# Moving the first LoRA factors to GpSimd's queue, with block 1's loads behind block 0's on the other two

## The chip, the cores and the metric

The kernel runs on one core of one Trainium2 chip. The time is the device time of one execution in microseconds (us). A core has five engines that run their own instruction streams and wait for one another on semaphores: TensorE (PE, matrix products; its weight loads are listed as PEld), VectorE (DVE), ScalarE (ACT), GpSimd (POOL) and SyncE (SP). SP, ACT and POOL can request transfers between the chip's memory and the on-chip buffer; the transfers run on the core's 16 DMA engines. A request by SP or ACT is listed under SPq or ACTq.

## The reference

The input x has 2 sequences of 1024 tokens with 512 features. It is normalized over the features, passed through a state-space convolution along the features and, in parallel, through a gated feed-forward network with LoRA factors; their product is added to x. Cut to what matters here:

```python
xn = layernorm(x)                                    # over the 512 features
s  = s4_convolution(xn) + D * xn
h1 = xn @ w1.T + 2 * (xn @ A1.T) @ B1.T              # hidden size 1376, rank 16
h3 = xn @ w3.T + 2 * (xn @ A3.T) @ B3.T
h2 = silu(h1) * h3
g  = silu(h2 @ w2.T + 2 * (h2 @ A2.T) @ B2.T)
out = x + s * g
```

Everything is fp32.

## The kernel before

The 2048 tokens are cut into 4 blocks of 512 (TB), each of 4 tiles of 128 tokens (NTT). The hidden size 1376 is cut into 5 pairs of 256 columns and a last piece of 96 columns (LASTR). The large products run as block products of a fast matrix multiplication with 7 instead of 8 partial products on two levels, so sums and differences of weights and tokens are made on DVE and POOL, and PE runs chains of products, almost all at line L801.

The LoRA factors are not applied to the tokens. PE multiplies the factors A and B with each other (`lora_product`, L412), and the result times 2 is added to the weights (`merge`, L422, for a pair; `take_last` and `merge_last`, L522 and L530, for the last piece). The weights so merged then meet the tokens.

The order of the work is written out by hand: each engine runs its instructions in the order in which the program names them. Requests of transfers also run in the order of their queue. A request on SP or ACT takes one of eight semaphores in turn, so the ninth waits until the first has landed, and so on.

The start of the program, in the order of its lines:

- `load_x(0)` (L232, L238): the four tiles of block 0, 256 KB each, alternating between SP's queue (tiles 0 and 2) and ACT's (tiles 1 and 3).
- POOL clears `warm` and builds the identity `ident`, which PE needs for transposes.
- `load_lora` (L398 to L403) for the two factor pairs: each requests A (`lo_d`, 16 rows of 512) at L401 and columns 768 to 1375 of B (`lo_h`, 16 rows of 608) at L402. The first pair goes to SP's queue, the second to ACT's.
- ACT runs an activation on `warm` (L1031), which loads its function table.
- `load_x(1)`: the four tiles of block 1, all on SP's queue.
- POOL builds a triangle `tri`, used much later.
- SP's queue: the last piece of the weights (`load_last`, L504), pair 0 (`load_pair`, L431), blocks 2 and 3, pair 1, and a second copy of the factors.

Then the work: PE runs 18 + 18 products of the identity (`keep_warm`, L1049) and after them the LoRA products of the last piece (`lora_last`, into the y banks) and half of those of pair 0. ACT scales the first (L522). DVE takes the statistics of block 0 tile by tile (L254, L255), and makes the reciprocal root (L59 to L68) and the shift (L291). ACT normalizes tiles 0 and 2 (L300), POOL tiles 1 and 3 (L304). POOL then adds the scaled LoRA products to the last piece (L530). PE transposes block 0 (L311), ACT copies it out (L319), and the first chain runs on the last piece (L801). The same steps follow for block 1: statistics on DVE, normalization on ACT and POOL, transposes (L331). On ACT, L522 stands before L300; on DVE, block 1's statistics stand right behind block 0's shift.

Of the kernel before, what the change touches and what calls it, by code (L numbers as in the profile page):

```python
# [21 lines left out]
HID = 1376  # L22
# [11 lines left out]
LSPLIT = 6 * P  # L34
# [75 lines left out]
def s4_gated_ffn(  # L110
# [39 lines left out]
    nc = tc.nc  # L150
# [66 lines left out]
    def value(tag="s"):  # L217
        return upool.tile([P, TB], F32, tag=tag, name=tag, bufs={"s": 8, "c": 4}[tag])
# [13 lines left out]
    def load_x(b):  # L232
        room = (None, None, t_in[4], t_in[6])[b]
        tiles = []
        for tt in range(NTT):
            t = value() if room is None else room[:, tt, :]
            queue = nc.scalar if b == 0 and tt % 2 else nc.sync
            queue.dma_start(out=t, in_=x[bass.ds(b * TB + tt * P, P), :])  # L238
            tiles.append(t)
        return tiles  # L240
# [157 lines left out]
    def load_lora(queue, group, d, h, lo, hi):  # L398
        rows = slice(32 * group, 32 * group + R)
        if d is not None:  # L400
            queue.dma_start(out=lora["d"][rows, :], in_=d)  # L401
        queue.dma_start(out=lora["h"][rows, : hi - lo], in_=h[:, lo:hi])  # L402
        lora["base"][group] = lo  # L403
# [607 lines left out]
    def add_chain(n, ch, places=PLACES):  # L1011
# [8 lines left out]
        for i, p in places:  # L1020
            at(7 * n + p, lambda i=i: step(i))

    x_in = {0: load_x(0)}
    warm = const.tile([P, 1], F32, name="warm")
    nc.gpsimd.memset(warm, 0.0)
# [1 line left out]
    lora_tiles(LSPLIT)  # L1027
    factors = (a1, b1T), (a3, b3T)
    for v, f in enumerate(factors):
        load_lora((nc.sync, nc.scalar)[v], v, *f, LSPLIT, HID)  # L1030
    nc.scalar.activation(warm, warm, AF.Silu)  # L1031
    x_in[1] = load_x(1)
    make_upper_triangular(nc, tri, 1.0, diag=True)
    w_last, s_last = load_last()
    w_pair, s_pair = {0: load_pair(0)}, {c: {} for c in range(NPAIR)}
    x_in[2], x_in[3] = load_x(2), load_x(3)
    w_pair[1] = load_pair(1)
    for v, f in enumerate(factors):
# [90 lines left out]
    for n in range(4):  # L1129
        half, v = 1 - n // 2, n % 2  # L1130
# [19 lines left out]
    for n, place in enumerate((10.7, 11.7, 13.7, 14.4)):  # L1150
        b, i = divmod(n, 2)
# [517 lines left out]
```

## Time and profile before

| what | value |
|---|---|
| median of 3 runs | 437.12 us (437.03 to 437.62) |
| the profiled execution's own time | 437.84 us |
| its span (first to last instruction) | 435.8 us |
| PE busy | 429.5 us, 99% of the span |
| DVE, POOL, ACT busy | 324.0, 210.8 and 146.4 us |
| moved by DMA | 53.60 MB, mean 123 GB/s |

The profile is one execution; its time is 2.04 us above its span, and 0.72 us above the median of the runs. Times in it count from the start of the span. A row of the timeline gives the start, the busy time, the engine, the line, the operation, the tiles written and read, the shapes and the number of instructions merged; in brackets stands the idle time just before and what ended it. A row of the chain of waits gives the start, the duration and the work that the end depended on. A row of DMA issues ends with the size and the time from the request to the landing. A row of stretches gives the granted clock, then for PE, PEld, DVE, ACT and POOL the busy time and the number of instructions, the clock again, the mean busy share of the 16 DMA engines and GB/s.

In the first 36 us the transfers are dense: the DMA engines are busy 80 to 100% of the time from about 2 to 24 us.

### The profile page before, as it was taken

The numbers are of one execution on the slowest core, as the hardware profiler recorded it, in microseconds if no ns is written. First come the engines' busy times: TensorE is split into PE (matmuls) and PEld (weight loads), VectorE is DVE, ScalarE is ACT, GpSimd is POOL, SyncE is SP. The second block draws the span as 40 slices with busy tenths as digits, with TensorE's granted clock in tenths as the row PEclk, the third lists the DMA queues.
The fourth block names the chain that finished last, engine by engine and source line by source line (L and its number), as shares of the span: only waits on it lengthen the run. The fifth ranks groups of instructions, "written<-read, shape, count | busy, mean of one in ns | idle before, by whom it ended". The sixth has DMA issues, their size and how long they took to land.

```text
span 435.8 us, 5085 instructions
## 1 busy us (share of the span) xinstructions
PE 429.5 (99%) x1664; PEld 270.6 (62%) x1664; DVE 324.0 (74%) x531; ACT 146.4 (34%) x301; POOL 210.8 (48%) x159
## 2 busy tenths in 40 slices
PE   7999999999999999999999999999999999999996
PEld 7645334444444444444443447888898999989996
DVE  5989998995894789478946788879786885753234
ACT  2897243443254325432543242211101212112221
POOL 1629186699689467946794478300000123222221
PEclk9999999999999999999999999999999999999999
DMA  7930313026015101521154554495902832423211
GB/s 242 367 100 21 137 49 101 0 73 194 25 37 170 60 25 46 167 67 31 49 157 158 168 166 154 125 352 194 350 2 78 307 118 96 146 96 98 74 72 48
DMA packets 35465, 53.60 MB, mean 123 GB/s; under 512 B 4688, under 2 KB 21520, under 8 KB 35312
## 3 DMA queue, kind: packets, MB, share of 16 engines
q1 hardware_dynamic: 31824, 49.55, 34.1%
q10 hardware_dynamic: 3616, 3.74, 2.9%
q8 instruction: 13, 0.21, 0.2%
q14 instruction: 12, 0.10, 0.1%
HBM read 33.88 MB, written 19.40 MB: 122 GB/s over the span
## 4 chain that ended last, share of the span: by engine, by line
PE 88%; DVE 8%; ACT 1%; DMA 1%; issue 1%; POOL 0%; SPq 0%; DVEq 0%; ACTq 0%; POOLq 0%
PE x L801 43%; PE y L801 23%; PE w L801 12%; PE aux L982 2%; PE w L982 2%; PE aux L997 2%; DVE xt L357 2%; DMA s<-in_x_dram 1%; DVE s L487 1%; PE y L412 1%; DVE w L475 1%; PE y L574 1%; PE aux L756 1%; ACT c L261 1%; DVE aux L1384 1%
## 5 line engine op out<-in xcount | busy, mean ns | idle before, releaser
L1387 POOL TENSOR_TENSOR o<-o,xin 128x512 f32<-128x512 f32 (+1 forms) x17 | 23.3, 1368 | 132.7 <-DVE o L1386 132.7
L887 POOL TENSOR_TENSOR s<-c,s 128x512 f32<-128x512 f32 (+1 forms) x44 | 67.0, 1526 | 20.1 <-ACT c L879 17.5
L821 ACT COPY s<-x 128x512 f32<-128x512 f32 (+1 forms) x54 | 31.6, 586 | 76.4 <-PE x L801 72.1
L801 PE MATMUL x<-t_in,s 128*128 128x512 f32 (+1 forms) x148 | 55.5, 495 | 0.0
L825 DVE TENSOR_TENSOR s<-s,y 128x512 f32<-128x512 f32 (+1 forms) x54 | 36.5, 681 | 15.3 <-ACT s L821 8.4
L921 POOL TENSOR_TENSOR s<-ua_three,s 128x512 f32<-128x512 f32 x20 | 35.0, 1751 | 14.7 <-DVE s L825 14.7
L801 PEld LDWEIGHTS x<-t_in,s 128*128 128x128 f32 x148 | 27.6, 190 | 20.9 <-issue 17.9
L801 PE MATMUL y<-t_in,s 128*128 128x256 f32 (+1 forms) x108 | 36.4, 461 | 0.0
L921 POOL TENSOR_TENSOR ua_three<-ua_three,s 128x512 f32<-128x512 f32 x20 | 29.5, 1477 | 12.3 <-DVE s L825 12.3
L1409 ACT COPY z<-x 128x256 f32<-128x256 f32 x24 | 8.8, 372 | 69.6 <-PE x L801 69.5
L1384 DVE TENSOR_TENSOR aux<-aux,m 128x384 f32<-128x384 f32 x32 | 18.1, 565 | 15.7 <-PE aux L982 14.1
L921 POOL TENSOR_TENSOR s<-u_three,s 128x512 f32<-128x512 f32 x20 | 26.7, 1333 | 3.7 <-DVE s L825 1.8
L801 PEld LDWEIGHTS y<-t_in,s 128*128 128x128 f32 x108 | 19.8, 190 | 11.7 <-issue 7.3
L879 ACT ACTIVATE c<-c 128x512 f32<-128x512 f32 x40 | 24.1, 630 | 8.9 <-DVE c L921 8.9
L844 ACT COPY w<-x 128x512 f32<-128x512 f32 (+1 forms) x37 | 21.1, 571 | 15.7 <-PE x L801 15.7
L475 DVE TENSOR_TENSOR w<-w 128x512 f32<-128x512 f32 x20 | 22.5, 1138 | 0.1
L921 POOL TENSOR_TENSOR u_three<-ua_three,u_three 128x512 f32<-128x512 f32 x10 | 13.0, 1302 | 16.9 <-DVE u_three L825 15.5
L801 PE MATMUL x<-xt,w 128*128 128x512 f32 x40 | 20.6, 597 | 0.0
L801 PE MATMUL x<-xr,w 128*128 128x512 f32 x40 | 20.6, 597 | 0.0
L801 PE MATMUL x<-xr,s 128*128 128x512 f32 x40 | 20.4, 596 | 0.0
L801 PE MATMUL x<-xt,s 128*128 128x512 f32 x40 | 20.4, 592 | 0.0
L801 PE MATMUL x<-t_in,w 128*128 128x512 f32 x40 | 20.4, 592 | 0.0
(321 smaller groups left out, 922.0 us busy)
## 6 DMA issues: line engine op xcount, KB each, us to landing
g_dram<-s SPq DMA_DIRECT2D x40, 256.0 KB, 2.1
g<-g_dram SPq DMA_DIRECT2D x10, 512.0 KB, 6.4
xin<-in_x_dram SPq DMA_DIRECT2D x16, 256.0 KB, 2.8
out_dram<-o SPq DMA_DIRECT2D x14, 256.0 KB, 2.0
t_in<-g_dram SPq DMA_DIRECT2D x6, 512.0 KB, 4.2
t_in<-in_x_dram SPq DMA_DIRECT2D x8, 256.0 KB, 5.5
w_a<-in_w2T_dram SPq DMA_DIRECT2D x2, 1024.0 KB, 7.1
room<-g_dram SPq DMA_DIRECT2D x4, 512.0 KB, 5.6
```

Source lines behind the costliest of these rows:

```text
L475: nc.vector.tensor_tensor(*sums[name])
L801: nc.tensor.matmul(ps[:, cols], lhsT=lhsT, rhs=rhs if parts == 1 else rhs[:, cols], start=first and i == 0 and part == 0, stop=i == len(pa ...
L821: nc.scalar.copy(t, self.x)
L825: nc.vector.tensor_tensor(t, t, self.y, add)
L844: nc.scalar.copy(self.w, self.x)
L879: nc.scalar.activation(c, c if src is None else src, AF.Silu)
L887: nc.gpsimd.tensor_tensor(g, act, g, mult)
L921: (nc.vector if o < 20 else nc.gpsimd).tensor_tensor(to, a, b, add)
L982: nc.tensor.matmul(to[:, n * P : (n + 1) * P], lhsT=x_, rhs=by, start=start, stop=True, skip_group_check=True,)
L1384: nc.vector.tensor_tensor(y[:, P:], y[:, P:], m[:, n * P : (n + 3) * P], add)
L1387: (nc.vector if last else nc.gpsimd).tensor_tensor(o, o, self.xin[h][:, cols], add)
L1409: nc.scalar.copy(t, xb)
```

## The change

Three edits, all at the start of the program. The two pairs of factors are requested on POOL's queue, behind the identity and before the triangle. Block 1's four tiles are requested alternately on SP's and ACT's queue, like block 0's. `load_x(1)` is placed before the activation on `warm`, so that ACT's two requests for block 1 stand before its table load. The order on PE and DVE is the same; on POOL four requests are added; on ACT two requests of factors are replaced by two of block 1; on SP two requests of factors and two of block 1 are gone, and those of block 1 that remain follow block 0's without a wait, since with fewer requests before them they take free semaphores.

```diff
@@ load_x
-            queue = nc.scalar if b == 0 and tt % 2 else nc.sync
+            queue = nc.scalar if b < 2 and tt % 2 else nc.sync
@@ after make_identity
     lora_tiles(LSPLIT)
     factors = (a1, b1T), (a3, b3T)
     for v, f in enumerate(factors):
-        load_lora((nc.sync, nc.scalar)[v], v, *f, LSPLIT, HID)
-    nc.scalar.activation(warm, warm, AF.Silu)
+        load_lora(nc.gpsimd, v, *f, LSPLIT, HID)
     x_in[1] = load_x(1)
+    nc.scalar.activation(warm, warm, AF.Silu)
     make_upper_triangular(nc, tri, 1.0, diag=True)
     w_last, s_last = load_last()
```

More of the change, by code (lines that the diff above doesn't have):

```diff
@@ L1029, in s4_gated_ffn @@
     for v, f in enumerate(factors):
-        load_lora((nc.sync, nc.scalar)[v], v, *f, LSPLIT, HID)
+        load_lora(nc.gpsimd, v, *f, LSPLIT, HID)
+    x_in[1] = load_x(1)
     nc.scalar.activation(warm, warm, AF.Silu)
-    x_in[1] = load_x(1)
     make_upper_triangular(nc, tri, 1.0, diag=True)
```

## The prediction

> **What bounds the kernel now.** First the page: its shares say who is busy, its chain who sets the end.
>
> ```profile
> span 435.8 us, 5085 instructions
> PE 429.5 (99%) x1664; PEld 270.6 (62%) x1664; DVE 324.0 (74%) x531; ACT 146.4 (34%) x301; POOL 210.8 (48%) x159
> PE 88%; DVE 8%; ACT 1%; DMA 1%; issue 1%; POOL 0%; SPq 0%; DVEq 0%; ACTq 0%; POOLq 0%
> ```
>
> TensorE (PE) is the bound, 88% of the chain; transfers hold 1%. Nearly all loads of this kernel are hidden, so the diff can pay only where PE has not yet begun its unbroken run. I looked for that place in the timeline, and then followed the chain of waits of the first 21 us.
>
> ```profile
> 7.82 1.04 PEld L412 LDWEIGHTS y<-lo_h,lo_d 16*128 16x128 f32 x15 [0.22 <-issue]
> 8.98 0.87 ACT L522 ACTIVATE c<-y 128x384 f32<-128x384 f32 x2 [4.90 <-PE y L412]
> 10.31 1.52 ACT L300 ACTIVATE s<-s,shift,rs_y 128x512 f32<-128x512 f32 x2 [0.46 <-DVE shift L291]
> 11.18 1.09 PE L311 MATMUL aux<-ident,s 128*128 128x128 f32 x8 [1.15 <-ACT s L300]
> 18.76 1.02 PE L801 MATMUL w<-xr,last 128*96 128x512 f32 x2
> 20.47 1.88 PE L801 MATMUL y<-xt,last 128*96 128x512 f32 x4
> ```
>
> From 18.76 on PE starts a 512-column product every 0.43 us (two rows later, at 20.47, four begin 1.71 after two pairs), with gaps of tenths only. So the end is 18.76 plus a nearly fixed 417 us, and the change is worth what it moves 18.76. Back from there PE is also dense down to 11.18, where it had idled 1.15 us for ScalarE's (ACT's) normalization of block 0. That began at 10.31, and two strands meet in it.
>
> ```profile
> 1.16 5.41 DMA s<-in_x_dram
> 6.59 0.71 DVE stats L254
> 10.12 0.17 DVE shift L291
> 10.31 0.82 ACT s L300
> ```
>
> Strand one, which ends last: block 0's third tile releases VectorE (DVE) at 6.59; from there to the shift's end is a fixed 3.70 us of small operations (6.59 to 10.29). Strand two: the first LoRA factors, which L412 multiplies from 7.82; L522 on ACT waits for them and ends at 8.98 + 0.87 = 9.85, and since ACT runs in order L300 stands behind it. The slack of this strand is 10.31 - 9.85 = 0.46 us. Their landings:
>
> ```profile
> s<-in_x_dram ACTq DMA_DIRECT2D x1, 256.0 KB, 5.7
> lo_d<-in_a_dram ACTq DMA_DIRECT2D x1, 32.0 KB, 5.9
> lo_h<-in_b3T_dram ACTq DMA_DIRECT2D x1, 38.0 KB, 5.8
> ```
>
> The last factor is requested at 2.11 and lands 5.8 later, at 7.91, which is where PE begins L412. PE's weight loads had been free since 7.82 - 0.22 = 7.60, when the warming products ran out: earlier factors gain 0.2 us at most.
>
> **What is removed.** Four factor requests leave the two hardware queues (0.42 to 0.45 us of issue each). The third tile of block 0 should profit. The stretches of one microsecond show why it is late:
>
> ```profile
> 4.00:5.00 1.00, 1.00 (x7) 1.00 (x7) 0.97 (x3) 0.08 (x1) 0.00 (x0) 1.00 1.01 357
> 5.00:6.00 1.00, 1.00 (x7) 1.00 (x7) 0.59 (x2) 0.00 (x0) 0.00 (x0) 1.00 0.70 93
> 6.00:7.00 1.00, 1.00 (x12) 1.00 (x11) 0.41 (x1) 0.00 (x0) 0.00 (x0) 1.00 1.04 232
> ```
>
> The last two columns are the DMA engines' share and GB/s. Stretches 1 to 5 us carried 43, 371, 385 and 357 GB/s, 1.16 MB in all; block 0 is 1.05 MB. So its bytes had mostly moved by 5.0, yet the release came at 6.57, after a stretch in which the engines were 70% busy for 93 GB/s. In that stretch the factors' rows (16 partitions, 0.14 MB) are what stands behind block 0 on both queues. If they are the reason, up to 6.59 - 5.63 = 0.96 us can go (5.63 is when DVE has finished the first two tiles); if not, nothing. I take half: 0.5, so the release is at 6.1 and the shift ends at 9.8.
>
> **What is added.** Four requests on GpSimd (POOL), in order after the identity's last operation, which ends at 1.02 + 0.29 = 1.31; two operations for the triangle stand behind them and are needed much later, and POOL's next work is at 10.38. The trace has no POOL request. Below, the issue is bounded by the hardware queues' 0.43 us; above by the longest mean POOL row, 1.75 us (L921, 128x512). From issue to landing, below: 1.9 us, the median of the late 48 KB factors on a quiet queue; above: 5.8, theirs now, behind block 0. On a queue of their own they stand behind nothing, so I take 2.1 near the lower end, and 1.1 for the issue, the middle of its bounds. The last factor then lands at 1.31 + 4 x 1.1 + 2.1 = 7.8: L412 starts at 7.8, L522 ends 2.0 later (7.85 to 9.85 now), at 9.8, and the slack holds. The bounds run from 1.31 + 1.7 + 1.9 = 4.9 (held by PE's 7.60) to 1.31 + 7.0 + 5.8 = 14.1.
>
> [...]
>
> **What is moved.** Block 1's four requests stand fifth to eighth in line. Now they wait for block 0's landings and leave SP between 3.91 and 7.39; then they leave both queues by about 2.5 (two requests ended at 1.57 to 1.60, two more take 0.9). ACT still issues four requests before its table load at 2.59, so the warm activation does not move. Block 1's bytes follow block 0's: 2.1 MB at the 371 GB/s of the second stretch, from 2.0, is 7.7, some 9 with a landing delay of 1; DVE first needs them at 10.20 - 0.5 = 9.7. Covered by DVE's own 3.70 us on block 0; without that cover it would cost microsecond for microsecond.
> On SP the two "last" loads (L504) then wait for tiles 0 and 1 and go near 4 instead of 7.43, the weights, blocks 2 and 3 and the second pair up to 3 us sooner. No engine's wait in the first 36 us ends on any of them, so I price this at nothing; the cover is POOL's normalization, which ends at 11.91 while the "last" pieces land at 11.3 and 12.0. A faster start would have eaten that cover; the earlier requests restore it.
>
> **The sum.** L300 starts at the later of 9.8 (shift) and 9.8 (L522), about 9.85 instead of 10.31: 0.46 us gained. PE, ACT and DVE follow in order, so 18.76 becomes 18.3, and the span 435.8 - 0.45 = 435.35. The profiled execution took 437.84, 2.04 more than its span; the median of the runs is 437.12, so I apply the difference there: **436.7 us**. A measurement of this kernel can tell about 0.2%, 0.87 us, from no change: the forecast lies within it.
>
> **Rivals.**
> *The factors become the bound (slower).* Place: L412, then L522 before L300 on ACT. Break-even is L412 at 10.31 - 2.04 = 8.27; from there each microsecond of lateness is one of time, and a loss of 0.87 needs a landing at 9.15. With 1.75 us per request and the quiet landing it is 1.31 + 7.0 + 1.9 = 10.2; midway, 9.7, L300 starts at 11.74: 1.43 lost, **438.6**. For it: four requests in one instruction stream, at an unknown price. Against: with the landing of 2.1 a request may take up to (8.27 - 1.31 - 2.1) / 4 = 1.2 us before anything is lost, and 1.43 before it shows. Chance 0.33.
> *Block 0 gains nothing.* The factor rows do not vanish; on a third queue they fall into block 0's own stream, and block 1 runs right behind. Then the release stays near 6.6 or moves back by their bytes' time, 0.14 MB at 371 GB/s = 0.4 us: 437.1 to 437.5, say **437.2**. Chance 0.14.
> *All of it comes through (faster).* Release at 5.63, factors before 7.60: L522 ends at 9.60, L300 starts at 9.64, 0.67 gained; DVE and POOL are then 0.96 ahead and may take up to 0.25 of the 0.53 us that PE's loads wait before L331. **436.2**. Against: it needs every step at its best. Chance 0.17.
> *The forecast*, a gain of 0.2 to 0.87: chance 0.36, the likeliest; its own range is 436.3 to 436.9.
>
> **How the numbers follow.** Within 0.2%: forecast and second rival, 0.50. Slower: 0.33. Faster: 0.17. Range 436.1 to 438.6: it takes in the fast rival and the slow one to its middle; beyond are the worst issue prices (above, some 0.15) and little below.
>
> **What would show it.** Right: block 0's third tile releases DVE at about 6.1; POOL's four requests take about 1.1 us each; L412 starts at 7.6 to 7.9; ACT's L300 starts near 9.85; block 1's tiles never release DVE; PE's product now at 18.76 begins at 18.3. Wrong: L522 waits for PE past 9, or ACT's L300 is released by L522 and not by the shift (first rival); DVE's third statistic still begins at 6.6 (second); a request on GpSimd of more than 1.2 us would alone overturn the sign, and of more than 1.43 us the verdict.

## The result, and the profile after

| | before | after |
|---|---|---|
| median (range, executions) | 437.31 us (436.73 to 437.85, 6) | 441.89 us (440.78 to 442.80, 6) |
| the profiled execution: time, span | 437.84, 435.8 us | 442.36, 440.5 us |
| mean granted clock of PE, all executions | 1.0 in the profiled one | 0.990 to 0.996 |

The change costs 4.6 us between the medians; the ratio is 1.0094, with a 95% interval of 1.0075 to 1.0112, which makes it 4.1 us. The forecast was 436.7, no change; its range ended at 438.6. The place is that of the first rival, the factors; the reason it gave, a dear issue, was not the cause, and its price was too small.

The page of the kernel after, busy times, slices and the chain by engine:

```profile
span 440.5 us, 5090 instructions
PE 432.4 (98%) x1664; PEld 272.9 (62%) x1664; DVE 324.9 (74%) x531; ACT 146.4 (33%) x301; POOL 213.0 (48%) x163
PEclk9699999999999999999999999999999999999999
PE 84%; DVE 7%; DMA 5%; ACT 1%; issue 1%; SPq 0%; POOL 0%; DVEq 0%; ACTq 0%; POOLq 0%
```

The line of the clock on the page before:

```profile
PEclk9999999999999999999999999999999999999999
```

PE has 2.9 us more busy time for the same 1664 products, and the second slice (11 to 22 us) shows the granted clock at six tenths; before, every slice had 9. So some of the loss is not waiting but products that take longer. The timeline of the same execution says where each part begins:

```profile
1.46 0.70 POOL L401 DMA_DIRECT2D lo_d<-in_a_dram  x1
...
3.13 0.49 POOL L402 DMA_DIRECT2D lo_h<-in_b3T_dram  x1
...
5.67 0.66 DVE L254 BATCH_NORM_STATS2 stats<-s 128x6 f32<-128x512 f32 x1
...
8.73 0.43 PE L412 MATMUL y<-lo_h,lo_d 16*128 16x96 f32 x2 [1.25 <-DMA lo_h<-in_b1T_dram]
9.57 0.69 DVE L254 BATCH_NORM_STATS2 stats<-s 128x6 f32<-128x512 f32 x1 [0.25 <-DMA s<-in_x_dram]
...
10.64 0.99 PE L412 MATMUL y<-lo_h,lo_d 16*128 16x96 f32 x13 [1.48 <-DMA lo_h<-in_b3T_dram]
...
11.59 0.87 ACT L522 ACTIVATE c<-y 128x384 f32<-128x384 f32 x2 [7.49 <-PE y L412]
...
12.35 1.51 ACT L300 ACTIVATE s<-s,shift,rs_y 128x512 f32<-128x512 f32 x2
13.21 1.97 PE L311 MATMUL aux<-ident,s 128*128 128x128 f32 x8
```

Read from the bottom. The transposes at L311 begin at 13.21 instead of 11.18, 2.03 us late, and eight of them take 1.97 instead of 1.09. L300 begins at 12.35 instead of 10.31, since ACT had 7.49 us with nothing to do ahead of L522, which waited for PE's L412; and PE waited twice for the factors, 1.25 us for the first `lo_h` and 1.48 us for the second. Block 0 is not the reason: its third statistic begins at 5.67 without a wait (6.59 before), and L300 could have begun near 9.3. The issues on POOL are cheap, 0.70 us once and then 0.49. What is long is the landing, the last number of each row of DMA issues:

```profile
lo_d<-in_a_dram POOLq DMA_DIRECT2D x2, 32.0 KB, 6.6
lo_h<-in_b1T_dram POOLq DMA_DIRECT2D x1, 38.0 KB, 6.4
lo_h<-in_b3T_dram POOLq DMA_DIRECT2D x1, 38.0 KB, 7.4
```

The last factor is requested at 3.13 and lands 7.4 later, at 10.53; before, on ACT's queue, it landed at 7.91, 5.8 after its request. The stretches of one microsecond show the second part of the loss, in the last column but two (the granted clock):

```profile
11.00:12.00 1.00, 1.00 (x17) 1.00 (x17) 0.93 (x5) 0.41 (x2) 0.00 (x0) 1.00 1.10 339
12.00:13.00 1.00, 1.00 (x6) 0.36 (x3) 0.93 (x4) 1.00 (x3) 0.84 (x2) 0.52 1.10 348
...
18.00:19.00 1.00, 1.00 (x4) 0.71 (x3) 0.00 (x0) 0.00 (x0) 0.93 (x2) 0.57 1.04 378
19.00:20.00 1.00, 1.00 (x8) 0.56 (x8) 0.00 (x0) 0.30 (x1) 0.76 (x2) 1.00 1.09 360
```

From 12.0 to 18.9 us PE runs at half clock, just where its dense run starts. To size the two parts I set, from the two traces, the starts of the same 1604 products of PE, from L311 on, against each other, after minus before:

```
first product (L311)                  +2.03 us
grows from 13.2 to 18.8 us to         +4.58 us
last product, 436.42 - 431.94         +4.48 us
```

So 2.0 us are lateness, 2.5 us are half clock, and behind 18.8 us nothing more is lost or won. In the chain DMA has grown from 1% to 5%: followed back from 59 us it now runs through block 1's tile (landing at 9.55) and requests behind it. This does not contradict the products: their distance does not move in that stretch.

### The profile page after: what moved, and what is told of

Read it like the earlier page. It is cut to its first block, busy times and chain, and to the rows that moved or that the text cites. A ratio compares the mean times of both kernels' runs of the same rounds, so it can differ in the third digit from the quotient of the medians.

```text
span 440.5 us, 5090 instructions
## 1 busy us (share of the span) xinstructions
PE 432.4 (98%) x1664; PEld 272.9 (62%) x1664; DVE 324.9 (74%) x531; ACT 146.4 (33%) x301; POOL 213.0 (48%) x163
## 4 chain that ended last, share of the span: by engine, by line
PE 84%; DVE 7%; DMA 5%; ACT 1%; issue 1%; SPq 0%; POOL 0%; DVEq 0%; ACTq 0%; POOLq 0%
PE x L801 42%; PE y L801 22%; PE w L801 11%; PE w L982 2%; PE aux L982 2%; DMA s<-in_x_dram 2%; PE aux L997 2%; DVE xt L357 2%; DMA w<-in_w3T_dram 1%; DMA t_in<-in_x_dram 1%; DMA lo_h<-in_b3T_dram 1%; DVE s L487 1%; PE y L412 1%; DVE w L475 1%; PE y L574 1%
## 5 line engine op out<-in xcount | busy, mean ns | idle before, releaser
L921 POOL TENSOR_TENSOR ua_three<-ua_three,s 128x512 f32<-128x512 f32 x20 | 29.5, 1476 | 12.3 <-DVE s L825 12.3
```

Of the source, the lines that this page charges most:

```text
L921: (nc.vector if o < 20 else nc.gpsimd).tensor_tensor(to, a, b, add)
```

## The experiments

The expectations speak of two theories for the late landing. Q: rows requested on GpSimd's queue come to be moved only when the hardware queues (SP's, ACT's) run low, so it is what stands there that makes them late. S: such a request is slow by itself, whatever else moves. Beside these stands the clock: that 2.5 us come from PE falling to half clock while it waits. Times of before differ between groups, since each is measured beside its own runs of before.

### Which part of the change costs: e1, e2, e3 and e4

**e1**, after, but block 1 all on SP's queue, right behind block 0 (the alternation undone). Of the change the move of the factors is left, and an earlier place of `load_x(1)` that leaves the order on every queue as it would be without it.

```diff
-            queue = nc.scalar if b < 2 and tt % 2 else nc.sync
+            queue = nc.scalar if b == 0 and tt % 2 else nc.sync
```

> The changed kernel, but block 1's four requests all go to SyncE's queue again (factors stay on GpSimd's). Theory Q (the factors' rows, requested in good time, wait in the DMA engines behind blocks 0 and 1): with block 1 on one ring only, less stands beside them while they wait, so the last factor lands earlier than the 10.5 us of the changed kernel, at 7 to 9.5, and the time falls to 437 to 440. Theory S (a request from GpSimd takes 6 to 7 us to land whatever else moves): the factors land at 10 to 11 as in the changed kernel, 441 to 442.

Measured: 441.52 us (440.45 to 441.85), before 437.92; ratio 1.0070 (1.0042 to 1.0097). The DMA issues and the timeline of e1:

```profile
lo_h<-in_b3T_dram POOLq DMA_DIRECT2D x1, 38.0 KB, 6.8
```

```profile
0.72 2.79 SPq L238 DMA_DIRECT2D s<-in_x_dram  x6
10.06 0.99 PE L412 MATMUL y<-lo_h,lo_d 16*128 16x96 f32 x13 [1.10 <-DMA lo_h<-in_b3T_dram]
```

The last factor lands 0.6 us sooner than in after, L311 begins 1.45 us late, and the half clock comes again (0.50 from 12 to 13 us): 3.8 us at the last product. So the move of the factors costs 3.6 us by itself, between the medians. It moves block 1 too. In the trace of before the requests of SP and ACT name eight semaphores in turn; the first eight leave without a wait, and block 1's four, the ninth to twelfth, leave from 3.91 to 7.39, SP waiting twice and 3.2 us in all for block 0's landings. In after GpSimd's four requests name four other semaphores. Without the factors, blocks 0 and 1 are the first eight of SP and ACT, and in e1 SP's six requests are out by 3.5 us. The alternation adds 0.6 us in the profiled executions (4.48 against 3.84 at the last product); the intervals do not separate the two runs. By the numbers expected this run spoke for S: the time lies in S's range, and the landing, at 9.9 us, is past Q's.

**e2**, after with the factors back on the hardware queues: block 1 alternating, behind them.

```diff
-        load_lora(nc.gpsimd, v, *f, LSPLIT, HID)
+        load_lora((nc.sync, nc.scalar)[v], v, *f, LSPLIT, HID)
```

> The kernel before with only the second half of the change: block 1's requests alternate between SyncE's and ScalarE's queue, the factors stay on these queues ahead of them. Both theories put the loss on the factors' landing: they land at about 7.9 as before, the clock stays full, and the time is 436.8 to 437.8, with ScalarE's table load some 4 us later but done before its first use. If block 1's place alone were the cause, it would be above 439.

Measured: 437.48 us (436.90 to 439.23), before 437.92; ratio 0.9993 (0.9971 to 1.0015). The timeline of e2 says what was tested:

```profile
3.99 2.36 SPq L238 DMA_DIRECT2D s<-in_x_dram  x2
4.18 2.64 ACTq L238 DMA_DIRECT2D s<-in_x_dram  x2
```

With the factors back, eight requests stand ahead of block 1 on the eight semaphores, and block 1 leaves from 4.0 to 6.8 us, nearly as late as before. The alternation costs and brings nothing while block 1 is held so. A block 1 that goes early behind factors on the hardware queues is in no run.

**e3**, after with more warming products, meant to keep PE busy until the factors land.

```diff
-        keep_warm(ps, 9, True)
+        keep_warm(ps, 24, True)
```

> The changed kernel with 48 warming products in place of 36 on TensorE (24 into each bank, not 9 in the changed kernel's 18 each row of the trace), so that it works until the last factor is there. Theory K (part of the loss is TensorE's clock, which fell to half from 12.4 to 18.6 us after the idle time): the clock stays full, and 2 to 2.7 us of the 4.6 come back: 439.0 to 440.0. If the lateness alone is the loss, the time stays at 441 to 442.5.

Measured: 444.07 us (443.49 to 446.20); ratio 1.0141 (1.0106 to 1.0175). A miss of mine: one warming product is two rows of the profile, so this is 96 rows and not 48; they ran until 15.0 us, and L311 came 6.5 us late. It says one thing all the same: in its profile the distance does not grow behind L311 (+6.5, at the end +6.2), as it did in after. PE had not waited for the factors, and in this execution nothing was lost to the clock; one of the four, at 446.20 us, had a mean clock of 0.996. e5 repeats it with the right number.

**e4**, before, with the later factor requests on GpSimd's queue, meant for a time when few other transfers run.

```diff
-                load_lora(nc.sync, group, None, h, 0, LSPLIT)
+                load_lora(nc.gpsimd, group, None, h, 0, LSPLIT)
```

> The kernel before, with the four late factor requests of 48 KB (some 30 us in, where little else moves) issued from GpSimd instead of SyncE; they are not urgent. Theory Q: about 0.5 us of GpSimd each, and a landing 2 to 3.5 us after the request. Theory S: 5 to 7 us to land here too. Time as before within 0.5 us.

Measured: 437.76 us in one execution. The DMA issues of e4, and for the same requests on SP's queue, of before; then the timeline of e4 and that of before:

```profile
lo_h<-in_b1T_dram POOLq DMA_DIRECT2D x2, 48.0 KB, 3.3
lo_h<-in_b3T_dram POOLq DMA_DIRECT2D x2, 48.0 KB, 4.9
```

```profile
lo_h<-in_b1T_dram SPq DMA_DIRECT2D x2, 48.0 KB, 1.9
lo_h<-in_b3T_dram SPq DMA_DIRECT2D x2, 48.0 KB, 2.0
```

```profile
42.06 1.20 POOL L402 DMA_DIRECT2D lo_h<-in_b1T_dram  x2
```

```profile
29.45 0.78 SPq L402 DMA_DIRECT2D lo_h<-in_b1T_dram  x2
```

The two do not compare like with like. SP issued these requests from 29.5 us on, with the DMA engines at most 41% busy; GpSimd reached them in its order of work at 42.06, and from 43 to 48 us the engines were 82 to 110% busy, mostly with SP's transfers. The landings of 3.3 and 4.9 us, 1.4 and 2.9 longer than on SP, thus hold some of the path by GpSimd and some of the load, and e4 does not part them. What it shows of the path is that its first row moves 1.8 us after the request (42.06 to 43.82), though the engines were 9% busy from 42 to 43 us. Of Q's expectation the first figure held; S's 5 to 7 us were not reached.

### The clock: e5

**e5**, after, with 16 instead of 9 warming products on each bank.

```diff
-        keep_warm(ps, 9, True)
+        keep_warm(ps, 16, True)
```

> The changed kernel with 32 warming products on TensorE in place of 18 (each product of 128 columns is two rows of the trace), which should end near 10.3 us, just before the last factor; the 48 of the run before overshot to 14. Theory K (part of the loss is TensorE's clock at half speed after the idle time): the clock stays full, L412 and all that follows start as late as in the changed kernel, and 1.5 to 2.5 us of its 4.6 come back: 439.0 to 440.4. If lateness alone is the loss: 441 to 442.5 as the changed kernel.

Measured: 440.19 us (439.74 to 440.27), before 437.52; ratio 1.0053 (1.0036 to 1.0071). The timeline of e5, and its stretch from 13 us:

```profile
1.37 9.12 PE L1049 MATMUL w<-ident 128*128 128x128 f32 x64 [1.37 <-POOL ident masks.py:199]
...
10.43 1.13 PE L412 MATMUL y<-lo_h,lo_d 16*128 16x96 f32 x16
...
12.35 1.51 ACT L300 ACTIVATE s<-s,shift,rs_y 128x512 f32<-128x512 f32 x2
13.22 1.09 PE L311 MATMUL aux<-ident,s 128*128 128x128 f32 x8 [0.76 <-ACT s L300]
```

```profile
13.00:14.00 1.00, 0.78 (x7) 0.79 (x8) 0.93 (x3) 0.95 (x3) 1.00 (x3) 1.00 1.10 366
```

The factors land as late as in after (7.2 us after the request), and L300 and L311 begin at the same times to 0.01 us. But PE is busy until the factors are there, the clock is 1.0 in all six executions, and the eight transposes take 1.09 us again. The last product is 1.79 us late instead of 4.48. The half clock is thus shown as a cost of its own: 2.5 us in the profiled executions (4.58 - 2.03), 1.7 in the medians (441.89 - 440.19), or 1.9 with each taken against its own before; the profiled one of after had the lowest clock of its six.

### What makes the landing late: e6 and e7

**e6**, e2 with the factor requests ahead of block 0 on SP's and ACT's queue.

```diff
+    lora_tiles(LSPLIT)
+    factors = (a1, b1T), (a3, b3T)
+    for v, f in enumerate(factors):
+        load_lora((nc.sync, nc.scalar)[v], v, *f, LSPLIT, HID)
     x_in = {0: load_x(0)}
```

> The other way to free block 0 of the factors' rows behind it: the factors are requested on SyncE's and ScalarE's queues ahead of block 0, block 1 alternates behind block 0. All theories: the factors land by 4 us, long before TensorE is free at 7.6, block 0's third tile is released at about 6.0, L300 starts at 9.6 to 9.9 against 10.3, the clock stays full: 0.3 to 0.7 us faster than before, 436.4 to 437.0 against 437.3. Unless block 0 comes later by the factors' 0.4 us and their slow rows, which would eat it: then 437.2 to 437.8.

Measured: 438.97 us (437.86 to 439.75), before 437.52; ratio 1.0022 (1.0006 to 1.0038). The timeline of e6, and its stretch from 12 us:

```profile
5.06 0.69 DVE L254 BATCH_NORM_STATS2 stats<-s 128x6 f32<-128x512 f32 x1 [5.06 <-DMA s<-in_x_dram]
...
10.37 1.52 ACT L300 ACTIVATE s<-s,shift,rs_y 128x512 f32<-128x512 f32 x2 [1.08 <-DVE shift L291]
...
11.24 1.53 PE L311 MATMUL aux<-ident,s 128*128 128x128 f32 x8 [1.96 <-ACT s L300]
```

```profile
12.00:13.00 1.00, 1.00 (x7) 1.00 (x6) 0.96 (x3) 0.73 (x2) 1.00 (x2) 0.50 1.10 350
```

Ahead of everything, the same factors land in 2.1 to 2.6 us; block 0's first tile then comes at 5.06 instead of 3.92. L311 begins with before's to 0.06 us, and yet the last product is 1.4 us late: PE, done with the factors by 9.3, waits 1.96 us for L300 and falls to half clock, as it did in 9 of the 12 executions (mean clock 0.996). Neither range expected holds. An idle PE costs here even when the transposes begin no later.

**e7**, before with the four factor requests on GpSimd's queue, and four requests of 4 bytes in their old places on SP and ACT, so that block 1 is held by the semaphores as before.

```diff
-        load_lora((nc.sync, nc.scalar)[v], v, *f, LSPLIT, HID)
+        load_lora(nc.gpsimd, v, *f, LSPLIT, HID)
+    row = const.tile([P, 4], F32, name="row")
+    for n in range(4):
+        (nc.sync, nc.scalar)[n // 2].dma_start(out=row[:1, n : n + 1], in_=x[n : n + 1, :1])
```

> Only the factors move to GpSimd's queue; block 1 stays as before, and four requests of 4 bytes stand in the factors' old places on the hardware queues, so that block 1 waits for block 0's landings as before and leaves near 4 us. Theory Q (the rows wait behind the hardware queues' rows): with only block 0 in line, the last factor lands at 6.5 to 8.3, and the time is 436.6 to 437.6. Theory S (slow path whatever moves): it lands at 9.5 to 10.5, TensorE idles and loses its clock, 440 to 442.

Measured: 438.08 us (437.34 to 439.40), before 437.52; ratio 1.0008 (0.9992 to 1.0024). The DMA issues of e7, then its timeline:

```profile
lo_h<-in_b1T_dram POOLq DMA_DIRECT2D x1, 38.0 KB, 5.0
lo_h<-in_b3T_dram POOLq DMA_DIRECT2D x1, 38.0 KB, 4.4
```

```profile
7.47 1.22 PE L412 MATMUL y<-lo_h,lo_d 16*128 16x96 f32 x15
...
9.67 1.52 ACT L300 ACTIVATE s<-s,shift,rs_y 128x512 f32<-128x512 f32 x2
...
10.54 1.09 PE L311 MATMUL aux<-ident,s 128*128 128x128 f32 x8 [0.84 <-ACT s L300]
```

The timeline of e7 on SP's queue:

```profile
3.94 2.80 SPq L238 DMA_DIRECT2D s<-in_x_dram  x4
```

This is the experiment that decides, and its pair is e1. The requests on GpSimd are the same as in e1 and in after, at the same times (1.46 to 3.13), and block 1 goes by SP in e1 and e7 alike; but in e7 the small requests hold the semaphores, and block 1 leaves from 3.9 us on as before, not by 3.5. The last factor lands at 7.5 instead of 9.9 (10.5 in after), L311 begins at 10.54, and the clock of the profiled execution stays 1.0; three of the ten had 0.996. S, which expects the late landing here too, falls; the median, 438.08, is 0.5 above what Q expected. With e1 it says: moving the factors costs because it lets block 1 go early, beside them. With block 1 held, the four landings by GpSimd's queue still took 4.4 to 5.3 us; in e6, ahead of everything on SP's and ACT's queue, they took 2.1 to 2.6. The view of the DMA queues shows the rows themselves, for 5.3 to 10.6 us of after and 4.5 to 5.0 of e7 (packets, MB, share of the 16 engines):

```profile
q1 hardware_dynamic: 1290, 0.85, 64.7%
q10 hardware_dynamic: 285, 0.52, 34.0%
q0 software_dynamic: 128, 0.14, 10.3%
```

```profile
q0 software_dynamic: 78, 0.10, 55.4%
```

In after no packet of q0, GpSimd's queue, moves before 5.3 us, 3.9 us after the first request, and all 128 then share the engines with block 1, half of whose bytes (q10, 0.52 MB) come by ACT's queue. In e7 q0's packets also move from 4.5 us on only, when block 0 is nearly through, but then they hold 55% of the engines. By the single packets of the traces, the factors' rows move from 5.4 to 10.0 us in after, from 4.9 to 9.3 in e1 and from 4.7 to 6.2 in e7: the start differs by less than 1 us, and the rest is that they move slowly among block 1's rows. So they do not wait until the hardware queues have run low, as Q has it, but what stands there makes them late. The landing of the last factor orders the cases by what stands in the hardware queues: 4.4 us (e7, block 1 held), 6.8 (e1, on one queue), 7.4 (after, on two). How the 16 engines choose between the queues no run shows; Q stands as far as that order goes, which is one profile for each case. From 5.4 us on, in after, the rows of q0 move between those of the other two queues; why none moves in the 3.9 us before, no run shows.

### Is there a version that gains? e8, e9 and e10

Each of these adds warming products before the transposes of block 0, against an idle PE: **e8** to e2 (4 products), **e9** to before (5), **e10** to e7 (4).

```diff
-    transpose(0, range(NTT), numbered("aux0", "aux1", "y0", "y1"))
+    banks = numbered("aux0", "aux1", "y0", "y1")
+    keep_warm(banks[0], 4, True)
+    transpose(0, range(NTT), banks)
```

> Run e2 (factors on the hardware queues, block 1 alternating) with 4 more warming products on TensorE between the LoRA products and block 0's transposes, where it idled 0.8 to 1.4 us. Theory K: that idle time is what lets the clock fall in some executions (4 of 13 to 9 of 25 of the kernel before, by the granted clock of 0.994 to 0.996), so here all executions show 1.0 and the slower ones vanish; with L300 about 0.5 us earlier the median is 436.4 to 437.2, 0.2 to 1.0 us under the kernel before. If the idle time does not matter: executions at 0.996 in the same share, median as before within 0.4 us.

> The kernel before with nothing but 5 such bridging products (1.07 us, in an idle time of 1.15 to 1.3 us). Theory K: all executions at a granted clock of 1.0; fast ones as before (436.8 to 437.9), none above 438.4, median 0.1 to 0.6 us under the kernel before. If not: a third of the executions at 0.996 and 1.5 us longer, as before.

> Run e7 (only the factors on GpSimd's queue, block 1 held back as before) with 4 bridging products before block 0's transposes. Theories Q and K together: the factors land at 7 to 8.3, L300 starts at 9.6 to 10.0, no execution below a clock of 0.998: median 436.5 to 437.2, 0.2 to 0.8 us under the kernel before. If the start gains less than it seems from single profiles: median within 0.2 us of the kernel before.

| | median (range) of 12 | before | ratio (95%) |
|---|---|---|---|
| e8 | 437.31 (436.96 to 437.67) | 437.44 | 0.9989 (0.9977 to 1.0001) |
| e9 | 437.54 (437.11 to 437.93) | 437.44 | 0.9997 (0.9986 to 1.0007) |
| e10 | 437.58 (437.18 to 438.12) | 437.17 | 1.0008 (0.9998 to 1.0017) |

None is shown to be faster than before: each interval holds 1, and none of the three medians reached the range that theory K gave it. In the profile of e9 the bridge itself holds up the transposes, which begin 1.26 us after L300, against 0.87 in before. What the bridges do is narrow the scatter. The clock was at least 0.998 in all 36 executions. Of before's, 4 of 23 in the group of e8 and e9 had a mean clock of 0.996 and took 438.70 to 439.21 us, and 2 of 17 in that of e10 had 0.994 to 0.996; over all four groups it is 20 of 78.

## Why the prediction was wrong, step by step

- **What bounds the kernel: right, with one thing left out.** The end follows the start of the dense run, and behind 18.8 us the products keep their distance to 0.1 us. But the 7.58 us from L311 (11.18) to its start (18.76) were taken as given too, and with the clock at half from 12.0 to 18.9 us they became 10.12 (13.21 to 23.33); nothing in the working asks what PE's clock does when its start is late. That is 2.5 of the 4.5 us at the last product.
- **What is removed: the event came, half of the gain was in doubt and is not shown.** Block 0's third tile was there by 5.67, all of the 0.96 us that I called the most. But 6.59 was a late draw: in two other profiles with before's start (e4 and e9) the third statistic begins at 6.05 and 5.73. It begins at 5.65 to 5.74 in the four profiles of after, e1, e3 and e5, and at 5.95 to 6.07 in those of e2, e7, e8 and e10, in which the factors' rows move beside block 0's last, on whichever queue. That would be the second rival's mechanism, at 0.3 us, but 0.3 us is also what parts e4 and e9, so it is not shown; and none of e2, e7, e8 and e10 showed a gain over before.
- **What is added: the step that failed.** "On a queue of their own they stand behind nothing, so I take 2.1 near the lower end, and 1.1 for the issue". The issue was too dear (four took 2.17 us, not 4.4), the landing far too cheap: 6.4 to 7.4 us, beyond the upper end of 5.8 too. The sum put the last factor at 7.8; it came at 10.53. A price from a quiet stretch (1.9 us, SP's requests at about 30 us) was put on a stretch of which the prediction itself showed 350 GB/s. And the change made it worse: with the factors gone from the hardware queues, block 1's 1.05 MB stood there before the factors had moved. The prediction has block 1 leave by 2.5 us, in its next step, but never asks what that does to the factors. Of the 5.3 us by which the last landing was priced too low (7.4 - 2.1), 2.3 remain when block 1 is held (4.4 in e7), and 3.0 come with block 1.
- **What is moved: nearly right.** The requests of block 1 left early, as forecast; what that cost the factors stands above. That its tiles never release DVE was wrong by 0.25 us (at 9.57), off the path. The "last" pieces and the weights are not on it either. The landing delay of 1 us in that step was my estimate; in after the factors' rows were through at 10.0, and the last landing came at 10.53.
- **The sum and its break-even: nearly right.** Break-even was L412 at 8.27, with 2.04 us from there to L300. With L412's last run at 10.64 this gives a loss of 2.37; L300 came 2.04 later. Where all products of the y banks run behind the landing and L300 waits for L522 alone, in e3 and e5, it takes 1.92 us; in after, where two of them had run in the first gap, 1.71.
- **The first rival** had the chain (L412, L522, L300) right, at a third of the chance. Its price of 1.43 us came from the issue; with the measured landing and the clock it is 4.5.

## What to carry to other kernels

Price a request by what stands in the other queues when it is made, not by the queue it is put on: here a queue of its own did not keep the factors from moving among block 1's rows, from 5.4 to 10.0 us in after, against 4.7 to 6.2 in e7 with block 1 held. When a request leaves a queue, ask what it held back there: here its semaphores were what kept block 1 out of the way, which left from 3.9 us on in before and e7, and by 3.5 in e1. Price the steps of a change together. Where PE starts late after an idle gap, add what a lower clock would cost to the lateness (here 2.5 us to 2.0), and before calling a wait of one profile a gain to be had, see it in a second profile.

## What the runs showed of the hardware

PE's clock fell to half behind idle gaps of 1.1 to 2.0 us. In after PE idled 1.25 and 1.48 us with two products between, and the clock fell 1.4 us after the second gap, for 6.8 us (summed over the stretches: one at 0.52, five at 0.50, one at 0.57). In e1 the gaps were 1.31 and 1.10 us, and the half clock lasted as long. In e6 it fell behind one gap of 1.96 us, for 3.4 us, from 0.5 us after the gap. Behind gaps of 0.76 (e5) and 0.84 us (e7) it stayed at 1.0 in their profiles; behind before's own 1.15 us it did so in its profile too, but the executions of before with a mean clock of 0.994 to 0.996 are about 1.5 us longer, and bridging that gap (e9) left none of them in 12. By the gap before L311 in the profile, executions at 0.996 or below were 1 of 10 in e3 and e5 (0.76 us), 3 of 10 in e7 (0.84), 2 of 10 in e2 (1.03), 20 of 78 in before (1.15) and 9 of 12 in e6 (1.96); in after and e1 all ten were. The half clock lasted 6.8 us in after and 3.4 in e6; what sets these times no run shows, and no gap ahead of them was longer than 1.96 us. Nor does a run tell whether the light products beside the gaps (16 rows deep) help to hold the clock up. Counted without them, the time from the last warming product to the first transpose was 2.7 us in e5, 3.4 in before, 3.9 in e6 and 5.7 in after: the same order as that of the loss.
